# Token statistics two groups at a time, and an exchange of work between ScalarE and VectorE in a feed-forward block

## The chip, the cores and the metric

The kernel runs on one core of a Trainium2 chip as a single launch. The metric is device time in microseconds, the median of a few executions. A core has four compute engines with an instruction queue each, which works in order: TensorE (PE in the profile, its weight loads PEld), VectorE (DVE), ScalarE (ACT) and GpSimd (POOL). SyncE (SP) issues most DMAs. Engines wait for each other by semaphores alone.

## The reference

Two layers work on `x` of 64 images, 55 x 55 points, 96 channels.

```python
x = conv_out * x + bias + x                  # depthwise 25 x 25 taps, every third kept
t = x.reshape(64, 3025, 96)
t = t + attn(ln(t))                          # ln: mean and variance over the 96 channels
t = t + ffn(ln(t))
# attn: h = relu(bn1(t @ w1.T)); FFT over the 3025 tokens; an affine map and a relu on real and
#       imaginary part; inverse FFT; bn2(y @ w2.T)
# ffn:  h = relu(q16(q16(q8(t) @ q8(W1).T) + q8(b1))); q16(q16(q8(h) @ q8(W2).T) + q8(b2))
```

`q8` rounds to an 8-bit float with five exponent bits (fp8e5), `q16` to fp16. So in the feed-forward block (FFN) each matrix product is rounded to fp16, gets a bias, is rounded to fp16 again, and the hidden values are then rounded to fp8.

## The kernel before

The convolution comes first (to about 940 us): TensorE multiplies by Toeplitz matrices, VectorE and GpSimd finish the tiles, and the result goes to HBM. Then come 64 sequences, one per image. A sequence holds its 3025 tokens as 121 partitions x 25 groups x 96 channels in a tile `t`, laid out as two channel halves: `[121, 2, 25, 48]`.

Each sequence is a list of small tasks (`sequence`, from L334):

- load `t`; first layer norm: statistics of the 25 groups in five tasks (L350), then `layernorm_tasks` (L289); scale (L363, GpSimd), transpose (`pa`, L376), copy to SBUF (`tnt`, ACT), product with w1 (`ph`, L397) and relu (`h`, ACT), first DFT step (`pf`, L412), copy (`g`, ACT), a round trip through HBM (`gd` to `gt`)
- second DFT step (`px`, L478), three affine forms on ACT (L495), four comparisons on VectorE (L504) and two sums on GpSimd (L511), product with w2 (`pd`, L553, L563; copy `d` on ACT), inverse DFT (`pe`, L583; copy `e` on ACT; a round trip through HBM; `py`, L644), residual (L655, VectorE)
- second layer norm: statistics (L661), `layernorm_tasks` again, centre and quantise (`xc` L677, `xq` L686, GpSimd), transpose (`pq`, L695), copy (`tq`, ACT)
- FFN up, nine blocks of 128 hidden channels x 1008 tokens (1009 in the last third): product (`pu`, L718), cast to fp16 (`y16`, L727), bias and relu (`z16`, L730), quantise to fp8 (`hq`, L742)
- FFN down: product (`pw`, L762), cast (`o16`, ACT, L771), bias (L776, VectorE), residual (`ot`, L782, GpSimd), store.

The order of work is set by a planner, `ordered` (L134). Each task has an engine, a cost in us, tasks it follows, buffers that it makes and uses, and a place: its number in the list `PLACES` plus one per sequence. `ordered` plays the queues through with these costs and takes for each engine the ready task with the earliest place, within a margin; the tasks of all 64 sequences are then written out in the order of their planned starts. So a new cost or a new task list gives other orders on every engine. The SP queue takes its DMAs in the same order, and at the start of the sequences the last stores of the convolution are mixed in, one after every third task (L1097). `AHEAD` and `NAHEAD` (L52) say how many first tasks of the first two sequences are written out within the convolution: the load, the statistics and the layer norm.

Statistics: `bn_stats` sends 96 channels of one group through VectorE and writes six numbers: count, mean and sum of squared deviations of the even-numbered elements, and the same of the odd-numbered. GpSimd joins the two halves (`variance`, L295 to L306: five small instructions, and two more for the mean in the second layer norm). Then ScalarE takes the square root (L311) and variance plus epsilon (L312), VectorE inverts (L315), and GpSimd takes one Newton step in four instructions (L319 to L322).

Buffers that matter: `psw` gives two PSUM tiles for `px` and `pu`, `psn` four for all other products; `y16` and `z16` have two buffers each, `hq` one, `stc` one.

Of the kernel before, what the change touches and what calls it, by code (L numbers as in the profile page):

```python
# [14 lines left out]
AF = mybir.ActivationFunctionType  # L15
ALU = mybir.AluOpType
# [21 lines left out]
CHH = CH // 2  # L38
# [9 lines left out]
KH, KHP = 31, 32  # L48
KC = 8
UPT = 1008  # L50

AHEAD, NAHEAD = 2, 10  # L52
# [5 lines left out]
    -0.85, -0.814, -0.754, -0.694, -0.634, -0.574, -0.232, -0.28, -0.28, -0.28, -0.26146, -0.13246,  # L58
    -0.13246, 0, 0, 0.074, 0.05, 0.06623, 0.06623, 0.14023, 0.11623, 0.15385, -0.129, 0, 0, 0.13246,
    0.13246, 0.20646, 0.18246, 0.19869, 0.19869, 0.27269, 0.24869, 0.30769, 0.00346, 0.13246, 0.13246,  # L60
    0.26492, 0.26492, 0.33892, 0.31492, 0.33115, 0.33115, 0.40515, 0.38115, 0.46154, 0.13592, 0.26492,
    0.26492, 0.39738, 0.39738, 0.47138, 0.44738, 0.46361, 0.46361, 0.53761, 0.51362, 0.61538, 0.26838,
    0.39738, 0.39738, 0.52985, 0.52985, 0.60385, 0.57985, 0.59608, 0.59608, 0.67008, 0.64608, 0.76923,
    0.40085, 0.52985, 0.52985, 0.66231, 0.66231, 0.73631, 0.71231, 0.72854, 0.72854, 0.80254, 0.77854,
    0.92308, 0.53331, 0.66231, 0.66231, 0.79477, 0.79477, 0.86877, 0.84477, 1.07692, 0.72, 0.97, 1.22, 1.47,
    0.9, 0.9, 0.9, 0.9, 0.9, 0.9, 0.9, 0.9, 0.774, 0.774, 1.046, 1.046, 1.046, 1.046, 1.046, 1.046, 1.046,
    1.046, 0.92, 0.92, 1.192, 1.192, 1.192, 1.192, 1.192, 1.192, 1.192, 1.192, 1.066, 1.066, 1.514, 1.534,
    1.534, 1.584, 1.584, 1.584, 1.66, 1.68, 1.68, 1.73, 1.73, 1.73, 1.73333, 1.338, 1.338, 1.338, 1.338,
    1.338, 1.338, 1.338, 1.338, 1.212, 1.212, 1.484, 1.484, 1.484, 1.484, 1.484, 1.484, 1.484, 1.484, 1.358,
    1.358, 1.63, 1.63, 1.63, 1.63, 1.63, 1.63, 1.63, 1.63, 1.504, 1.504, 1.952, 1.972, 1.972, 2.022, 2.022,  # L70
    2.022, 2.098, 2.118, 2.118, 2.168, 2.168, 2.168, 2.23333, 2.477, 2.677, 2.677, 2.687, 2.743, 2.743,
    2.753, 2.809, 2.809, 2.819, 2.875, 2.875, 2.885, 2.941, 2.941, 2.951, 2.975, 2.927, 2.927, 2.927, 2.835,
    2.835, 3.235, 3.235, 2.856, 2.856, 3.256, 3.256, 2.877, 2.877, 3.277, 3.277, 2.898, 2.898, 3.298, 3.298,
    2.919, 2.919, 3.319, 3.319, 2.94, 2.94, 3.34, 3.34, 2.961, 2.961, 3.361, 3.361, 3.509, 3.54, 3.509,
    3.509, 3.59436, 3.62536, 3.59436, 3.59436, 3.67972, 3.71072, 3.67972, 3.67972, 3.78836, 3.81936,
    3.78836, 3.78836, 3.87372, 3.90472, 3.87372, 3.87372, 3.95908, 3.99008, 3.95908, 3.95908, 4.06772,
    4.09872, 4.06772, 4.06772, 4.15308, 4.18408, 4.15308, 4.15308, 4.23844, 4.26944, 4.23844, 4.23844,
    3.466, 3.466, 3.466, 3.266, 3.516, 3.74536, 3.74536, 3.74536, 3.54536, 3.79536, 3.83848, 3.83848,
    3.83848, 3.63848, 3.88848, 4.02472, 4.02472, 4.02472, 3.82472, 4.07472, 4.10232, 4.10232, 4.10232,
    3.90232, 4.15232,  # L80
# [4 lines left out]
def conv_attn_hybrid(ctx, tc, a, out, t1s, tb, gds, eds):  # L85
# [48 lines left out]
    def ordered(bufs):  # L134
# [93 lines left out]
        t=5, sta=2, stc=1, xa=2, tnt=2, h=3, g=3, gd=2, gt=4, m=2, ar=2, nc=2, d1=2, sm=3, sr=2, d=4, e=2, ed=2,  # L228
        e2=1, xc=2, xq=2, tq=1, hq=1, y16=2, z16=2, o16=2, ot=3, rstda=2, rstdc=2, mean=2, psn=4, psw=2,
# [59 lines left out]
    def layernorm_tasks(b, what, t, after, mean):  # L289
# [5 lines left out]
        def variance():  # L295
            st_ = live[st]
            d, v = box["d"], box["v"] = small("d", name), small("v", name)
            nc.gpsimd.tensor_tensor(d, st_[:, :, 1], st_[:, :, 4], ALU.subtract)
            nc.gpsimd.tensor_tensor(v, st_[:, :, 2], st_[:, :, 5], ALU.add)
            nc.gpsimd.tensor_tensor(d, d, d, ALU.mult)  # L300
            nc.gpsimd.tensor_scalar(d, d, CH / 4.0, None, ALU.mult)
            nc.gpsimd.tensor_tensor(v, d, v, ALU.add)
            if mean is not None:
                m = make(mean, "mean", [NJ, NR1])
                nc.gpsimd.tensor_tensor(m, st_[:, :, 1], st_[:, :, 4], ALU.add)
                nc.gpsimd.tensor_scalar(m, m, 0.5, None, ALU.mult)  # L306

        def root():
            v, s = box["v"], small("s", name)
            box["s"] = s  # L310
            nc.scalar.activation(s, v, AF.Sqrt, bias=eps, scale=1.0 / CH)  # L311
            nc.scalar.activation(v, v, AF.Identity, bias=eps, scale=1.0 / CH)  # L312
# [11 lines left out]
        new = [(mean, "mean")] if mean is not None else []  # L324
        k = task("POOL", 1.9 if new else 1.45, variance, after, new=new, use=[st])
        k = task("ACT", 0.57, root, [k])
# [3 lines left out]
    def sequence(b):  # L330
# [13 lines left out]
        for q in range(5):  # L344

            def stats(q=q):
                if q == 0:
                    make(sta, "sta", [NJ, NR1, 6])
                for g in range(5 * q, 5 * q + 5):
                    nc.vector.bn_stats(live[sta][:, g, :], live[t][:, :, g, :])  # L350

            after = [loaded] + ks[:1]
            new = [(sta, "sta")] if q == 0 else []
            ks.append(task("DVE", 0.8, stats, after, new=new, use=[t] if new else [t, sta]))
        rstd = layernorm_tasks(b, "a", t, ks, None)
# [284 lines left out]
        for q in range(5):  # L640
# [16 lines left out]
            def stats(q=q):  # L657
                if q == 0:
                    make(stc, "stc", [NJ, NR1, 6])
                for g in range(5 * q, 5 * q + 5):  # L660
                    nc.vector.bn_stats(live[stc][:, g, :], live[t][:, :, g, :])  # L661
# [5 lines left out]
            ks.append(task("DVE", 0.8, stats, [k] + ks[:1], new=new, use=[t] if new else [t, stc]))  # L667
        mean = ("mean", b)
        rstd = layernorm_tasks(b, "c", t, ks, mean)
        turned_ = []  # L670
        for i in range(7):
# [3 lines left out]
            def centre(xc=xc, g0=g0, ng=ng):  # L675
                x = make(xc, "xc", [NJ, 4, CH])
                nc.gpsimd.tensor_tensor(  # L677
                    halves(x[:, :ng]),
                    live[t][:, :, g0 : g0 + ng, :],
                    halves(spread(live[mean], g0, ng)),  # L680
                    ALU.subtract,
                )
# [21 lines left out]
            k = task("POOL", 0.9 if ng == 4 else 0.48, centre, [rstd], new=[(xc, "xc")], use=[t, mean])  # L704
# [4 lines left out]
        for s, k in np.ndindex(3, 3):  # L709
# [16 lines left out]
            def cast(pu=pu, y16=y16, n=n):  # L726
                nc.vector.tensor_copy(live[y16][:, :n], live[pu][:, :n])  # L727
# [11 lines left out]
            def quantised(s=s, k=k, n=n, n0=n0, z16=z16):  # L739
                if s == 0 and k == 0:  # L740
                    make(hq, "hq", None)
                nc.scalar.activation(  # L742
                    live[hq][:, k, n0 : n0 + n], live[z16][:, :n], AF.Copy, saturate=False
                )
# [3 lines left out]
            x = task("DVE", 1.14, cast, [x], use=[pu, y16])  # L748
# [478 lines left out]
```

## Time and profile before

| | |
|---|---|
| time, median of 3 runs | 4573.0 us (4572.97 to 4574.33) |
| the profiled execution | span 4570.5 us; the median stands 2.5 us over it |
| PE busy | 4227.5 us, 92% of the span |
| DVE, ACT, POOL busy | 3311.5, 2953.9, 3071.1 us (72, 65, 67%) |
| y16 cast, L727, DVE | 576 instructions, 1201 ns each |
| z16 bias, L730, DVE | 576, 731 ns |
| hq quantise, L742, ACT | 576, 1049 ns |
| statistics, L350 and L661, DVE | 3200, 242 to 243 ns |
| mean granted TensorE clock | 0.974 of full speed |

Busy time is the union of an engine's instructions. Consecutive instructions of an engine overlap a little in the records, so the distance from start to start is what one costs its queue. "Idle before" is the time an engine stood still ahead of an instruction, with what released it; "issue" is idle time in which it waited for nothing that the profile shows. The chain of waits goes back from the last instruction, at each step to what released it.

### The profile page before, as it was taken

Reading aid. Unit: us, or ns where it says so; the run is one execution under the profiler, and the core shown is the slowest. Engines: PE = TensorE matmul, PEld = TensorE weight load, DVE = VectorE, ACT = ScalarE, POOL = GpSimd, SP = SyncE. Lnnn points to the kernel's source line nnn. Section 1 sums busy time; section 2 is a strip of 40 time slices with the busy share of each in tenths; the row PEclk is TensorE's granted clock in tenths of the full one; section 3 lists DMA queues with packets and bytes.
Section 4 is the critical chain, followed back from the end, with each engine's and each line's share of the span. In section 5 each row is a group of like instructions: output and inputs, shape, how many; then the busy total and the mean of one; then the engine's idle time right before and its main releaser. Section 6 shows DMA issues by size and latency. Waiting matters only on the chain.

```text
span 4570.5 us, 194901 instructions
## 1 busy us (share of the span) xinstructions
PE 4227.5 (92%) x83314; PEld 3487.6 (76%) x83314; DVE 3311.5 (72%) x7344; ACT 2953.9 (65%) x5947; POOL 3071.1 (67%) x4196
## 2 busy tenths in 40 slices
PE   8999898949999999999999999999999999999996
PEld 8989898937777777777777777777777777777774
DVE  5444344424788888888788788888888888888877
ACT  2000000017788888888888888888888888888875
POOL 2667676725666777777677676677777777667765
PEclk9999999969999999999999999999999999999996
DMA  4788888876666666766666666666666666667662
GB/s 178 180 206 207 247 197 196 198 171 168 167 176 177 177 180 179 186 179 178 178 181 182 177 175 179 177 180 179 177 182 181 184 182 177 179 175 181 178 173 79
DMA packets 572901, 823.11 MB, mean 180 GB/s; under 512 B 61641, under 2 KB 470924, under 8 KB 570754
## 3 DMA queue, kind: packets, MB, share of 16 engines
q1 hardware_dynamic: 449094, 741.40, 60.0%
q10 hardware_dynamic: 107996, 60.19, 7.0%
q0 software_dynamic: 14944, 9.06, 1.1%
q8 instruction: 655, 10.73, 1.0%
q14 instruction: 212, 1.74, 0.1%
HBM read 419.45 MB, written 390.64 MB: 177 GB/s over the span
## 4 chain that ended last, share of the span: by engine, by line
PE 62%; DVE 9%; DMA 9%; ACT 8%; issue 6%; POOL 4%; SPq 2%; ACTq 1%; POOLq 0%; DVEq 0%
PE pl L1000 13%; PE pf L412 9%; PE ph L397 8%; PE px L478 6%; PE pd L553 6%; PE py L644 4%; PE pu L718 3%; PE pd L563 3%; PE pe L583 3%; PE pa L376 2%; DMA x<-in_xc_dram 2%; PE pw L762 2%; DVE y L727 2%; POOL xq L686 1%; ACT m L495 1%
## 5 line engine op out<-in xcount | busy, mean ns | idle before, releaser
L1000 PE MATMUL pl<-x,toep 128*64 128x96 f32 (+1 forms) x18432 | 793.3, 250 | 75.4 <-DVE buf L1008 30.9
L1000 PEld LDWEIGHTS pl<-x,toep 128*64 128x64 f32 (+1 forms) x18432 | 785.8, 137 | 82.7 <-DVE buf L1008 32.0
L727 DVE CAST y<-pu 128x1008 f16<-128x1008 f32 (+1 forms) x576 | 688.6, 1201 | 197.7 <-PE pu L718 195.3
L397 PEld LDWEIGHTS ph<-w1e,tnt 97*121 97x121 f32 x3200 | 546.1, 185 | 247.5 <-issue 65.5
L397 PE MATMUL ph<-w1e,tnt 97*121 97x192 f32 x3200 | 670.1, 332 | 44.1 <-ACT g L416 26.4
L742 ACT ACTIVATE hq<-z 128x1008 fp8e5<-128x1008 f16 (+1 forms) x576 | 600.6, 1049 | 163.5 <-DVE z L730 162.9
L412 PE MATMUL pf<-h,f 121*128 121x384 f32 (+1 forms) x1664 | 667.9, 486 | 22.6 <-ACT h L406 16.0
L504 DVE SCALAR_TENSOR_TENSOR m<-px,par,m 128x400 f32<-128x400 f32 x768 | 480.7, 626 | 261.6 <-ACT ar L495 183.7
L311 ACT ACTIVATE sm_s_a<-sm_v_a,eps 121x25 f32<-121x25 f32 x64 | 20.4, 318 | 898.3 <-DMA t<-buf 876.3
L363 POOL TENSOR_TENSOR xa<-shared,rstda 121x384 f32<-121x384 f32 (+1 forms) x364 | 283.2, 781 | 366.7 <-PE pa L376 360.8
L478 PE MATMUL px<-m,gt 50*64 50x50 f32 x24576 | 453.0, 220 | 48.8 <-issue 42.9
L511 POOL TENSOR_TENSOR sm<-ar,m 128x400 f32<-128x400 f32 x256 | 269.9, 1054 | 339.0 <-DVE m L504 294.6
L478 PEld LDWEIGHTS px<-m,gt 50*64 50x64 f32 x24576 | 413.7, 135 | 107.7 <-issue 90.1
L1008 DVE SCALAR_TENSOR_TENSOR buf<-pl,x 121x384 f32<-121x384 f32 (+1 forms) x336 | 270.9, 842 | 291.8 <-PE pl L1000 176.9
L416 ACT COPY g<-pf 128x384 f32<-128x384 f32 (+1 forms) x832 | 385.8, 468 | 127.1 <-PE pf L412 62.7
L1018 POOL TENSOR_TENSOR buf<-buf,cbias 121x768 f32<-121x768 f32 (+1 forms) x168 | 303.4, 1819 | 237.2 <-DVE buf L1008 184.9
L553 PE MATMUL pd<-w2e,sm 128*64 128x96 f32 x8192 | 412.7, 252 | 33.3 <-ACT g L416 19.4
L406 ACT ACTIVATE h<-ph 121x384 f32<-121x384 f32 (+1 forms) x832 | 389.5, 488 | 66.5 <-PE ph L397 59.5
L730 DVE TENSOR_SCALAR z<-y,b1q 128x1008 f16<-128x1008 f16 (+1 forms) x576 | 418.2, 731 | 11.3
L553 PEld LDWEIGHTS pd<-w2e,sm 128*64 128x64 f32 x8192 | 354.5, 138 | 79.6 <-ACT g L416 23.9
L412 PEld LDWEIGHTS pf<-h,f 121*128 121x128 f32 x1664 | 293.3, 192 | 93.0 <-ACT h L406 24.0
L782 POOL TENSOR_TENSOR ot<-shared,o 121x480 f32<-121x480 f32 x260 | 304.3, 1178 | 81.2 <-DVE o L776 81.2
(129 smaller groups left out, 8639.3 us busy)
## 6 DMA issues: line engine op xcount, KB each, us to landing
gd<-g SPq DMA_DIRECT2D x768, 192.0 KB
gt<-gd SPq DMA_DIRECT2D x512, 288.0 KB
x<-in_xc_dram SPq DMA_DIRECT2D x240, 384.0 KB
out_dram<-ot SPq DMA_DIRECT2D x320, 210.0 KB
ed<-e SPq DMA_DIRECT2D x384, 150.0 KB
shared<-t SPq DMA_DIRECT2D x52, 1050.0 KB
t<-buf ACTq DMA_DIRECT2D x137, 288.0 KB
t<-shared ACTq DMA_DIRECT2D x65, 288.0 KB
```

The source lines that it names most:

```text
L397: nc.tensor.matmul(x[:NJ, q * H : (q + 1) * H], live[tnt][:, g * NJ : (g + 1) * NJ], w1e, start=True, stop=True,)
L406: nc.scalar.activation(live[h][:, : nq * H], live[ph][:NJ, : nq * H], AF.Relu)
L412: nc.tensor.matmul(x[:, : nq * H], f1, live[h][:, : nq * H], start=True, stop=True)
L416: nc.scalar.copy(live[g][:, q0 : q0 + nq].rearrange("p q c -> p (q c)"), live[pf][:, : nq * H])
L478: nc.tensor.matmul(x[to : to + 64].rearrange("p (q r n) -> p q r n", q=2, r=2)[:, k2p, :, o : o + NR1], y[rows, k % KC, c0 : c0 + 64], m1[ ...
L504: nc.vector.scalar_tensor_tensor(live[out_], view(px)[:, :, 256 : 256 + KC * NR1], scale, live[than], ALU.mult, ALU.max)
L553: nc.tensor.matmul(y[k % 2][64 * k2p : 64 * k2p + 64, k // 2 * CH : (k // 2 + 1) * CH], full[:, k, 64 * k2p : 64 * k2p + 64], w2e[:, 0, :] ...
L727: nc.vector.tensor_copy(live[y16][:, :n], live[pu][:, :n])
L730: nc.vector.tensor_scalar(make(z16, "z16", [128, 1024], F16)[:, :n], live[y16][:, :n], b1q[:, k : k + 1], 0.0, ALU.add, ALU.max,)
L742: nc.scalar.activation(live[hq][:, k, n0 : n0 + n], live[z16][:, :n], AF.Copy, saturate=False)
L782: nc.gpsimd.tensor_tensor(halves(y), live[t][:, :, 5 * q : 5 * q + 5], halves(live[o16]), ALU.add)
L1000: nc.tensor.matmul(pl[p : p + width, cc * NBS : (cc + 1) * NBS], toep[:, c0 + g + cc, o : o + width], xts[n, c0, m + d][:, g + cc, :], sta ...
```

## The change

1. Statistics take two groups per instruction. The access pattern runs over channels and, innermost, over the two groups, so that even elements belong to one group and odd ones to the other: 13 instructions of 192 elements in place of 25 of 96. The 25th group is paired with itself. Mean and sum of squares then come out per group, and the tile is `[121, 26, 3]`.
2. `variance` goes from both layer norms. ScalarE's `root` reads the sums straight from the statistics tile, and `centre` on GpSimd reads the mean there. `stc` gets a second buffer, `mean` goes, `PLACES` loses the two entries of `variance`, and `NAHEAD` is 9 for 10.
3. FFN up: ScalarE casts `pu` from PSUM to fp16, and VectorE quantises `z16` to fp8. The bias between them stays on VectorE.
4. The planner's costs follow: the five statistics tasks 0.56 or 0.84 us for 0.8, `root` 0.45 for 0.57, the cast 0.95 (ACT) for 1.14 (DVE), the quantise 0.62 (DVE) for 0.95 (ACT).

```diff
-AHEAD, NAHEAD = 2, 10
+PAIRS = ((0, 2), (2, 5), (5, 7), (7, 10), (10, 13))
+AHEAD, NAHEAD = 2, 9
...
+    def pair_stats(st, t, i):
+        g0, ng = 2 * i, min(2, NR1 - 2 * i)
+        x = t[:, :, g0 : g0 + ng, :].rearrange("p h g c -> p h c g")
+        if ng == 1:
+            x = x.to_broadcast([NJ, 2, CHH, 2])
+        nc.vector.bn_stats(st[:, g0 : g0 + 2, :].rearrange("p g n -> p (g n)"), x)
...
-        def variance():
...
         def root():
-            v, s = box["v"], small("s", name)
-            box["s"] = s
-            nc.scalar.activation(s, v, AF.Sqrt, bias=eps, scale=1.0 / CH)
-            nc.scalar.activation(v, v, AF.Identity, bias=eps, scale=1.0 / CH)
+            m2 = live[st][:, :NR1, 2]
+            v, s = box["v"], box["s"] = small("v", name), small("s", name)
+            nc.scalar.activation(s, m2, AF.Sqrt, bias=eps, scale=1.0 / CH)
+            nc.scalar.activation(v, m2, AF.Identity, bias=eps, scale=1.0 / CH)
...
-        k = task("POOL", 1.9 if new else 1.45, variance, after, new=new, use=[st])
-        k = task("ACT", 0.57, root, [k])
+        k = task("ACT", 0.45, root, after, use=[st])
...
-                for g in range(5 * q, 5 * q + 5):
-                    nc.vector.bn_stats(live[stc][:, g, :], live[t][:, :, g, :])
+                for i in range(*PAIRS[q]):
+                    pair_stats(live[stc], live[t], i)
...
-                    halves(spread(live[mean], g0, ng)),
+                    halves(spread(live[stc][:, :, 1], g0, ng)),
...
-                nc.vector.tensor_copy(live[y16][:, :n], live[pu][:, :n])
+                nc.scalar.copy(live[y16][:, :n], live[pu][:, :n])
...
-                nc.scalar.activation(
-                    live[hq][:, k, n0 : n0 + n], live[z16][:, :n], AF.Copy, saturate=False
-                )
+                nc.vector.tensor_copy(live[hq][:, k, n0 : n0 + n], live[z16][:, :n], saturate=False)
...
-            x = task("DVE", 1.14, cast, [x], use=[pu, y16])
+            x = task("ACT", 0.95, cast, [x], use=[pu, y16])
...
-            hq_done[s, k] = task("ACT", 0.95, quantised, after, new=[(hq, "hq")] if first else [], use=[z16] if first else [z16, hq])
+            hq_done[s, k] = task("DVE", 0.62, quantised, after, new=[(hq, "hq")] if first else [], use=[z16] if first else [z16, hq])
```

## The prediction

> **What bounds the kernel now.** First the page, for how much of the span each engine works and what the chain that ended last is made of:
>
> ```profile
> PE 4227.5 (92%) x83314; PEld 3487.6 (76%) x83314; DVE 3311.5 (72%) x7344; ACT 2953.9 (65%) x5947; POOL 3071.1 (67%) x4196
> ...
> PE 62%; DVE 9%; DMA 9%; ACT 8%; issue 6%; POOL 4%; SPq 2%; ACTq 1%; POOLq 0%; DVEq 0%
> ```
>
> The change touches only the 64 sequences, so the stage is looked at alone. The table of windows (length, then busy time of PE, PEld, DVE, ACT, POOL, granted clock, DMA share, GB/s):
>
> ```profile
> 940.00:1000.00 60.00, 24.60 (x89) 18.62 (x89) 15.20 (x93) 12.97 (x32) 14.06 (x39) 0.66 0.76 167
> ...
> 2000.00:2500.00 500.00, 476.75 (x9069) 374.95 (x9068) 409.27 (x940) 417.18 (x841) 355.37 (x530) 1.00 0.69 179
> 2500.00:3000.00 500.00, 475.96 (x9160) 375.08 (x9160) 413.38 (x958) 417.48 (x842) 355.28 (x530) 0.99 0.68 179
> ...
> 4500.00:4570.50 70.50, 43.32 (x354) 26.78 (x346) 49.12 (x85) 36.21 (x56) 39.34 (x52) 0.65 0.24 73
> ```
>
> In the steady part TensorE is busy 95% of the time, ACT and DVE 83%, POOL 71%. From 1000 to 4500 us there are 556 casts L727, nine to a sequence: 61.8 sequences, 56.6 us each. The change takes no work from TensorE, so only its idle time can be won. Who ended that, by the waits from 1000 to 4500 us (total us, times, longest), and the longest waits of the other engines there:
>
> ```profile
> PE px L478 <- issue: 42.9, 52, 2.4
> PE pd L553 <- ACT g L416: 19.4, 30, 0.8
> ...
> PE ph L397 <- ACT e L592: 11.4, 29, 0.4
> PE pa L376 <- ACT g L416: 10.0, 1, 10.0
> ...
> ACT hq L742 <- DVE z L730: 146.5, 179, 4.1
> ...
> POOL sm_d_c L298 <- DVE stc L661: 74.3, 61, 8.6
> ```
>
> PE's waits that name "issue" come to 87 us (px 42.9, pd 15.4 and 11.8, pe 8.1, pw 5.3, pq 3.0); they often fall in the middle of a run of matmuls and no part of the change touches them. Waits for ACT come to 60 us (g 19.4 and 3.3, e 11.4, o 7.8 and 3.1, h 6.2, hq 3.4, d 3.3, tq 1.7, without the single 10.0), for POOL 7, for DVE some 9. Why ACT is late, a stretch of the chain of waits shows (start, us, what):
>
> ```profile
> 2033.37 0.97 DVE o L776
> 2034.35 1.12 DVE y L727
> 2035.47 0.56 DVE shared L655
> 2036.03 0.62 DVE z L730
> 2036.65 0.02 issue
> 2036.68 1.05 ACT hq L742
> ...
> 2039.33 0.49 ACT e L592
> 2039.82 0.04 issue
> 2039.87 0.91 PE ph L397 x4
> ```
>
> VectorE is late with the bias, ACT stands in `hq` for it, and the PSUM copies queued behind `hq` reach TensorE late. And the bias is late because of GpSimd, by the timeline:
>
> ```profile
> 2023.13 0.83 POOL L363 TENSOR_TENSOR xa<-shared,rstda 121x384 f32<-121x384 f32 x1
> 2023.17 1.06 DVE L730 TENSOR_SCALAR z<-y,b1q 128x1008 f16<-128x1008 f16 x1
> ```
>
> `z` starts 0.04 us after `xa` and ends 0.27 us after it, though its shortest record is 374 ns. Over the steady part `z` takes 0.48 us on average when it starts with POOL idle, 0.83 when POOL is at work (worked out from the timeline): it waits for the running GpSimd instruction.
>
> **The change, part by part**, per sequence of 56.6 us.
>
> *Statistics.* Ten `bn_stats` of a run take 1.69 us in the timeline and five 0.89: 0.16 us from start to start for 96 elements. DVE's rows of 400 and 1008 elements step by 0.54 and 1.12 us, 0.95 ns an element, so a pair of 192 takes 0.16 + 96 x 0.95 = 0.25 us. 50 x 0.16 = 8.0 us become 26 x 0.25 = 6.5: DVE -1.5. No row shows the pattern that jumps between two groups; should it run at half rate, a pair takes 0.43 us and the term is +3.2. I take full rate, since `residual` and `centre` already read split patterns at ordinary rates.
>
> *Variance and mean.* The ten rows L298 to L306 of the two norms come to 88.4 + 115.9 = 204 us: POOL -3.2 us. The path from the last statistics to the root loses 1.6 us. POOL's wait for `stc` (74.3 us, 1.2 a sequence) goes over to ACT, where `root` now waits for VectorE directly; before, the root started 2.3 us after the statistics. Behind it on ACT stand `h`, `g`, `d` and `o`, for which PE waits. Price 0 to 1.2 us of ACT; I take 0, as the planner moves `root` with its inputs, and keep 1.2 for the range.
>
> *Cast on ACT.* ACT's PSUM rows: `o` 564 ns for 480 elements; slopes 0.78 (tnt, 484 against 121) to 0.91 ns (h, 384 against 192). So 0.98 to 1.04 us for 1008, against 1.05 for `hq`: ACT -0.6 to 0. ACT no longer waits for `z` (146.5 us, 2.4 a sequence); it waits for `pu`, and through the two `y16` buffers for the `z` two blocks earlier.
>
> *Quantise on DVE.* The nearest rows are two fp8 casts from SBUF in the preparation, 384 elements 342 ns and 288 elements 291 ns: 0.53 ns an element and 138 fixed, 0.67 us for 1008, 0.59 from start to start. That it moves two elements per cycle suggests that it shuts GpSimd out, and is shut out, as `z` is. Bounds of its wait: 0 (POOL idle) and 1.05 us (a whole POOL row such as L511). `z` waits 0.36 (731 less 374); but the changed order puts `hq` directly behind its `z` in 352 of 576 cases, where POOL, held up by `z`, gets in between. The nearest row for that is `z` directly behind a bias L776: 0.87 us, a wait of 0.50. I take 0.5 to 0.6. Nine times: cast -9 x 1.12 = -10.1, quantise +9 x (0.59 + 0.55) = +10.3. DVE +0.2, from -4.8 to +4.7.
>
> *Sums.* DVE -1.3, ACT -0.3, POOL -3.2 plus what `hq` makes it stand (0 to 9 x 0.59 x 0.71 = 3.8; half of it, 1.9) = -1.3. No engine becomes the bound. The gain is in who waits for whom: ACT, which feeds TensorE, is cut loose from the VectorE to GpSimd contention, and `hq` on VectorE is needed only by `pw`, which waited 3.4 us in all. I take half of the 60 us that PE waits for ACT, since one of ACT's four large waits goes and the chain passes through it: -30 us. All of it, with POOL's 7, would be -67; nothing, 0.
>
> *A rule of the Trainium skill against this.* The row first: `z` above ends with the POOL instruction, 374 ns at best and 1326 at worst. "SBUF — State Buffer", section "Who interferes with whom", says the same as a rule: VectorE's two-port instructions and GpSimd hold a port pair exclusively for a whole instruction, and ScalarE never waits for anyone; so the move takes work from the engine that can't be blocked to one that can. By the rule's half of a POOL instruction the nine quantises would cost VectorE 9 x (0.59 + 0.5 x 0.71 x 1.0) = 8.5 us, by the row behind L776 10.3.
>
> *Ends.* From 940 to 1025 us the chain stands in SP's DMA queue (L1100) and PE does nothing; the same stores precede the first complete set of `gd` puts, with two of them later in between: 0, plus or minus 3. In the last 70 us the root comes 1.6 us earlier, and the last six FFN blocks, which step by 1.12 + 0.39 us on DVE, step by 0.39 + 0.59 there and 0.9 on ACT: 6 x 0.5 = 3.2. Some of it is lost to POOL: -4 (0 to -8).
>
> 4570.5 - 30 - 4 = 4536.5; with the 2.5 us by which the median stands over the span, **4539 us**, 0.7% faster.
>
> **The rivals.**
>
> - *Hidden anyway.* PE's idle time hardly moves, since what ended last was a tie of several late engines; the tail alone remains: 4573 - 5 = 4568. For it: TensorE is at 95%, and half of its idle time is "issue". Against: the chain through `hq` above.
> - *The contention decides: slower.* Place: the pairs `z`, `hq` on VectorE. VectorE's time stands even at a wait of (10.1 + 1.5) / 9 - 0.59 = 0.70 us per `hq`. At a whole POOL row, 1.05, it has 9 x 0.35 = 3.2 us more; `z` falls behind, `y16` is not free, ACT stands in the cast and PE behind ACT. One POOL row of 0.83 us (L363) on PE per sequence is 62 x 0.83 = +51: 4624. For it: after the change VectorE has 23 instructions a sequence that contend, for 14. Against: POOL has 3.2 us less to do.
> - *Another order, by chance worse.* All queues are planned anew with the old places. If PE's 1.2 us of waits on engines per sequence double, 76 us: 4649. Nothing in the profile speaks for a sign.
> - *The fp8 copy runs at one element per cycle.* Then 9 x 0.5 = 4.5 us more on DVE, as in the second rival; the two preparation rows speak against it.
>
> **How the numbers follow.** The forecast 0.52, hidden anyway 0.16, contention 0.22 (the slow copy in it), a worse order 0.10. About 0.2%, 9 us, is what a measurement tells from no change. Faster: 0.52 and a quarter of the hidden case, 0.56; within it: the rest of that, 0.12; slower: 0.32. The likeliest case alone runs from 4573 - 75 = 4498 (all 67 and 8 of the tail) to 4564. The range goes below it by a little, for waits that the view counts under other names, to 4492, and up to 4624, the price of contention, leaving the worse orders out: 0.05 below and 0.13 above.
>
> **What would show it.** `bn_stats` x1664 near 335 ns a record; `hq` on DVE 0.67 us at its shortest and 1.1 to 1.3 on average; the cast on ACT near 1.0; no wait ACT hq for DVE z; PE above 96% in the steady windows, and its waits for ACT near 30 us. It is wrong if ACT's cast waits for VectorE, if `root` waits for `stc` by more than 50 us in all, if `hq` averages over 1.45 us, or if PE's waits on DVE, 9 us now, grow past 40.

## The result: 5.6% slower, and the profile after

The changed kernel takes 4833.6 us (median; 4828.1 to 4835.3) against 4573.7 us beside it: a ratio of 1.056, 95% interval 1.0528 to 1.0592. The forecast was 4539 us, its range ended at 4624. Sign and range were both wrong. The profiled execution has a span of 4833.5 us, 263 us more than before.

The page of the changed kernel: the span, the busy times, and what the chain that ended last is made of.

```profile
span 4833.5 us, 192945 instructions
...
PE 4315.1 (89%) x83314; PEld 3562.8 (74%) x83314; DVE 3006.5 (62%) x5808; ACT 2933.5 (61%) x5947; POOL 2994.2 (62%) x3428
...
PE 61%; issue 9%; POOL 8%; DMA 8%; ACT 6%; DVE 5%; SPq 2%; ACTq 1%; POOLq 0%; DVEq 0%
```

DVE, ACT and POOL all have less to do than before (3311.5, 2953.9, 3071.1 us), and yet the whole takes longer. In the chain, POOL has doubled (4 to 8%), "issue" went from 6 to 9%. TensorE has the same 83314 matmuls and is busy 88 us more. The table of windows of the changed kernel (length, busy time of PE, PEld, DVE, ACT, POOL, granted clock, DMA share, GB/s) shows that it is the steady part that lost:

```profile
940.00:1000.00 60.00, 26.78 (x87) 19.44 (x86) 10.83 (x40) 12.95 (x32) 5.41 (x10) 0.66 0.78 150
2000.00:2500.00 500.00, 449.15 (x8373) 354.58 (x8371) 341.71 (x679) 381.72 (x774) 317.27 (x388) 0.96 0.63 163
2500.00:3000.00 500.00, 450.95 (x8175) 355.72 (x8172) 338.81 (x672) 376.10 (x765) 313.04 (x384) 0.95 0.64 164
```

TensorE's busy share fell from 95 to 90%, and its granted clock from 0.99 or 1.00 to 0.95 or 0.96. At the start of the sequences (940 to 1000 us) TensorE is about as busy as it was (26.78 us, 24.60 before). From 1100 to 4400 us a sequence (nine `z` records) takes 59.64 us, before 55.10. Of these 4.54 us, 3.02 are idle time of TensorE (5.61 for 2.59) and 1.52 are busy time (54.03 for 52.51); sixty times 4.54 us, 272 us, covers the whole loss. (The prediction's 56.6 us a sequence was an average that took in the slow start; it scaled only small terms.)

Who ended TensorE's idle time in the changed kernel, from 1050 to 4750 us (total us, times, longest):

```profile
PE px L472 <- issue: 101.9, 65, 4.7
PE pq L689 <- POOL xq L680: 42.0, 66, 1.5
PE pe L577 <- issue: 32.3, 21, 4.7
PE pw L754 <- DVE hq L736: 31.6, 32, 3.9
...
PE pd L547 <- ACT g L410: 8.0, 11, 1.2
```

Summed by releaser, and set against the kernel before from 1050 to 4500 us: "issue" 182 us (before 87), GpSimd 51 (7), VectorE 51 (11), ScalarE 51 (55). So three kinds of wait grew, and the waits for ScalarE, of which half should have gone, hardly moved.

The durations of the changed instructions, in contrast, came out close to what was foreseen or below it. Groups of VectorE in the changed kernel (busy us, mean ns of one, then the idle time ahead of them with its releasers):

```profile
L736 DVE CAST hq<-z 128x1008 fp8e5<-128x1008 f16 (+1 forms) x576 | 508.4, 886 | 12.5
...
L724 DVE TENSOR_SCALAR z<-y,b1q 128x1008 f16<-128x1008 f16 (+1 forms) x576 | 379.0, 661 | 348.6 <-ACT y L721 348.2
...
L295 DVE BATCH_NORM_STATS2 stc<-shared 121x6 f32<-121x192 f32 x676 | 197.9, 350 | 0.8
```

From the list of ScalarE's waits there, its `y16` cast (`y`), a copy (`tnt`) and the root of the second layer norm (`sm_s_c`):

```profile
ACT y L721 <- PE pu L712: 21.8, 28, 3.0
ACT tnt L375 <- PE pa L370: 15.6, 22, 1.6
ACT sm_s_c L306 <- DVE stc L295: 7.5, 10, 1.1
```

The cast is not held by VectorE, and that root waits 7.5 us for `stc` in all. The local steps of the change did what was expected of them; the whole did not.

### The profile page after: what moved, and what is told of

The parts are those of the page before. It is cut to its first block, busy times and chain, and to the rows that moved or that the text cites. A ratio compares the mean times of both kernels' runs of the same rounds, so it can differ in the third digit from the quotient of the medians.

```text
span 4833.5 us, 192945 instructions
## 1 busy us (share of the span) xinstructions
PE 4315.1 (89%) x83314; PEld 3562.8 (74%) x83314; DVE 3006.5 (62%) x5808; ACT 2933.5 (61%) x5947; POOL 2994.2 (62%) x3428
## 4 chain that ended last, share of the span: by engine, by line
PE 61%; issue 9%; POOL 8%; DMA 8%; ACT 6%; DVE 5%; SPq 2%; ACTq 1%; POOLq 0%; DVEq 0%
PE pl L992 12%; PE pf L406 8%; PE ph L391 7%; PE pd L547 7%; PE px L472 6%; PE py L638 4%; PE pd L557 4%; PE pu L712 3%; PE pe L577 3%; PE pw L754 3%; PE pa L370 3%; DMA x<-in_xc_dram 2%; DMA gt<-gd 2%; POOL xq L680 2%; POOL ot L774 2%
## 5 line engine op out<-in xcount | busy, mean ns | idle before, releaser
L992 PE MATMUL pl<-x,toep 128*57 128x96 f32 (+1 forms) x18432 | 790.3, 249 | 73.0 <-DVE buf L1000 32.4
L992 PEld LDWEIGHTS pl<-x,toep 128*57 128x57 f32 (+1 forms) x18432 | 781.6, 136 | 81.5 <-DVE buf L1000 33.5
L721 ACT CAST y<-pu 128x1008 f16<-128x1008 f32 (+1 forms) x576 | 581.5, 1013 | 29.5 <-PE pu L712 26.6
L724 DVE TENSOR_SCALAR z<-y,b1q 128x1008 f16<-128x1008 f16 (+1 forms) x576 | 379.0, 661 | 348.6 <-ACT y L721 348.2
L306 ACT ACTIVATE sm_s_a<-sta,eps 121x25 f32<-121x25 f32 x64 | 22.2, 347 | 880.2 <-DMA t<-buf 871.0
L736 DVE CAST hq<-z 128x1008 fp8e5<-128x1008 f16 (+1 forms) x576 | 508.4, 886 | 12.5
L410 ACT COPY g<-pf 128x384 f32<-128x384 f32 (+1 forms) x832 | 399.1, 481 | 136.5 <-PE pf L406 79.5
L547 PE MATMUL pd<-w2e,sm 128*64 128x96 f32 x8192 | 435.4, 261 | 42.2 <-issue 13.8
L547 PEld LDWEIGHTS pd<-w2e,sm 128*64 128x64 f32 x8192 | 377.1, 145 | 100.0 <-issue 37.0
L566 ACT COPY d<-pd 128x384 f32<-128x384 f32 x512 | 220.6, 483 | 316.0 <-PE pd L557 315.3
L680 POOL TENSOR_TENSOR xq<-xc,rstdc 121x384 fp8e5<-121x384 f32 (+1 forms) x448 | 367.9, 832 | 51.3 <-PE pq L689 50.0
```

The lines of the kernel that those rows point to most:

```text
L410: nc.scalar.copy(live[g][:, q0 : q0 + nq].rearrange("p q c -> p (q c)"), live[pf][:, : nq * H])
L547: nc.tensor.matmul(y[k % 2][64 * k2p : 64 * k2p + 64, k // 2 * CH : (k // 2 + 1) * CH], full[:, k, 64 * k2p : 64 * k2p + 64], w2e[:, 0, :] ...
L680: nc.gpsimd.tensor_tensor(x[:, :ng], live[xc][:, :ng], spread(live["rstdc", b], g0, ng), ALU.mult, saturate=False)
L721: nc.scalar.copy(live[y16][:, :n], live[pu][:, :n])
L724: nc.vector.tensor_scalar(make(z16, "z16", [128, 1024], F16)[:, :n], live[y16][:, :n], b1q[:, k : k + 1], 0.0, ALU.add, ALU.max,)
L736: nc.vector.tensor_copy(live[hq][:, k, n0 : n0 + n], live[z16][:, :n], saturate=False)
```

## The experiments

Two theories stood first. One: the changed operations cost the time (the contention rival of the prediction, by whatever path). Two: the order costs it, because every queue was planned anew from places that had been set for the old costs and tasks. An order and the operations in it can be taken apart here: if the planner is given the old costs and task list, the old order is written out, and the task bodies may still issue the new instructions on the new engines.

### All of the new operations in the old order

```diff
 # costs, task list, PLACES, buffer counts as the planner sees them: those of the kernel before
+        def variance():
+            pass
-        k = task("ACT", 0.45, root, after, use=[st])
+        k = task("POOL", 1.9 if new else 1.45, variance, after, new=new, use=[st])
+        k = task("ACT", 0.57, root, [k])
```

> All operations of the changed kernel, written out in the order that the planner made for the kernel before (it plans with the old task list, engines and costs; the two variance tasks stand in the plan and issue nothing). Order theory (the queues planned anew cost the time, the operations do not): 4540 to 4600 us. Contention theory (the fp8 quantise on VectorE and GpSimd hold each other up, so the operations cost the time): 4780 to 4850 us, as the changed kernel. TensorE's waits in the middle of a run of matmuls under issue: order theory about 80 us, as before; contention theory no statement.

Measured: 4689 us, ratio 1.0246 (1.021 to 1.0282). So 2.5% belongs to the operations even in the order that suited the kernel before, and the new order adds 1.056 / 1.0246 = 1.031, another 3.1%. The time lies between the two windows that were expected, and both theories hold a part. In this run TensorE waited 79.5 us for `xq` on GpSimd (6.9 before).

### The old operations in the new order

```diff
 # costs, task list and PLACES: those of the changed kernel
-                nc.scalar.copy(live[y16][:, :n], live[pu][:, :n])
+                nc.vector.tensor_copy(live[y16][:, :n], live[pu][:, :n])
-                nc.vector.tensor_copy(live[hq][:, k, n0 : n0 + n], live[z16][:, :n], saturate=False)
+                nc.scalar.activation(live[hq][:, k, n0 : n0 + n], live[z16][:, :n], AF.Copy, saturate=False)
 # root issues the five or seven GpSimd instructions of variance as before; bn_stats one group at a time
```

> The operations of the kernel before, written out in the order that the planner made for the changed kernel (variance stands directly ahead of the root). Order theory: 4780 to 4900 us, about as slow as the changed kernel or slower, as the casts are on an engine the plan did not mean. Contention theory: 4560 to 4640 us.

Measured: 5221 us, ratio 1.1408 (1.1345 to 1.1471), with a granted clock of 0.932. That is above both windows. The order made for the exchange is much worse for the old operations than for the new ones. The shares of order and operations therefore do not simply add: an order is good or bad for one assignment of work.

### The changed kernel with another margin of the planner

```diff
-    FULL, SWITCH, NEAR, RING = "128x128", 0.09, 0.359, 8
+    FULL, SWITCH, NEAR, RING = "128x128", 0.09, 0.2, 8
```

> The changed kernel with one number of the planner changed: the margin by which a ready task may run ahead of one with an earlier place, 0.2 for 0.359. All operations and costs stay; only the order differs. Order theory: the time moves by more than 40 us either way from 4834, and TensorE's idle time in the steady part moves with it. Contention theory: 4800 to 4870 us, since the same operations meet each other as often.

Measured: 4681 us (the median of 4654, 4681 and 4685; a fourth execution of 18392 us stands apart and is not in the ratio), ratio 1.0198 (1.0135 to 1.0261). One constant of the planner, with no instruction changed, wins 150 us back. So an order alone can carry some 3.5% (1.056 / 1.0198 = 1.035), no less than the step from the old order to the new one; the changed operations then take about what they take in the old order (1.0246).

### The kernel before with its margin moved

```diff
-    FULL, SWITCH, NEAR, RING = "128x128", 0.09, 0.359, 8
+    FULL, SWITCH, NEAR, RING = "128x128", 0.09, 0.37, 8
```

> The kernel before with the planner's margin 0.37 for 0.359; all operations and costs stay, only the order differs. If the order before was a fortunate one that any new planning loses: 4650 to 4850 us. If the order matters little: 4560 to 4610 us.

Measured: 4798 us, ratio 1.046 (1.0417 to 1.0504). Moving the margin by 0.011 costs the unchanged operations 4.6%. So the order of the kernel before is a fortunate one for its places: a small step of the margin leaves it. Only this one step was tried.

### The FFN exchange alone, in the old order

```diff
-                nc.vector.tensor_copy(live[y16][:, :n], live[pu][:, :n])
+                nc.scalar.copy(live[y16][:, :n], live[pu][:, :n])
-                nc.scalar.activation(
-                    live[hq][:, k, n0 : n0 + n], live[z16][:, :n], AF.Copy, saturate=False
-                )
+                nc.vector.tensor_copy(live[hq][:, k, n0 : n0 + n], live[z16][:, :n], saturate=False)
```

> The kernel before with the exchange in the feed-forward block alone (cast on ScalarE, quantise on VectorE) and with the order and statistics of before. Order theory: 4540 to 4610 us. Contention theory: 4750 us or more, as nothing of GpSimd's work has gone.

Measured: 4683 us, ratio 1.0232 (1.0196 to 1.0269): nearly all of the 2.5% is the exchange. The time lies between the windows of the two theories. TensorE's longest waits in this run, 1050 to 4500 us:

```profile
PE pq L695 <- POOL xq L686: 76.3, 108, 2.0
PE px L478 <- issue: 37.6, 44, 2.2
```

Before, the first of these was 6.9 us. Its cause stands in GpSimd's groups, same operations and same order, first in this run and then in the kernel before (1100 to 4400 us; the number after the busy time is the mean ns of one):

```profile
L686 POOL TENSOR_TENSOR xq<-xc,rstdc 121x384 fp8e5<-121x384 f32 x354 | 312.7, 890 | 1.4 <-PE pq L695 0.8 <-DMA gt<-gd 0.6
...
L511 POOL TENSOR_TENSOR sm<-d,nc 128x400 f32<-128x400 f32 x234 | 266.8, 1140 | 0.0
L363 POOL TENSOR_TENSOR xa<-shared,rstda 121x384 f32<-121x384 f32 x276 | 258.5, 939 | 239.8 <-PE pa L376 237.8 <-DMA gd<-g 0.2
```

```profile
L686 POOL TENSOR_TENSOR xq<-xc,rstdc 121x384 fp8e5<-121x384 f32 x362 | 305.9, 851 | 7.8 <-PE pq L695 7.6
...
L511 POOL TENSOR_TENSOR sm<-d,nc 128x400 f32<-128x400 f32 x240 | 248.5, 1035 | 0.0
L363 POOL TENSOR_TENSOR xa<-shared,rstda 121x384 f32<-121x384 f32 x291 | 247.9, 852 | 299.5 <-PE pa L376 293.8 <-PE pu L718 2.9
```

These three rows are 39 to 105 ns longer. Within this one trace the longer records are those that meet an `hq` in time: `sm` takes 1038 ns on average beside neither `hq` nor `z`, 1030 ns beside a `z` alone and 1480 ns beside an `hq` alone (137, 42 and 55 records, by the times of start and end). Per sequence the durations of GpSimd's records add up to 43.3 us for 40.4, +2.9. It works through `xc` and `xq` in one stretch, in which it hardly waits (1.4 us ahead of `xq` in all), and the transposes `pq` follow right behind it: there 1.2 of the 2.9 us a sequence turn into TensorE's wait. TensorE's idle time is 3.70 us a sequence for 2.59, and a sequence takes 56.79 us for 55.10. The exchange did also what it was forecast to do: TensorE's waits for ScalarE fell, from 54.5 to 30.7 us. But its waits for GpSimd rose from 6.9 to 76.3.

### The exchange with a quantise of 16 columns

```diff
-                nc.vector.tensor_copy(live[hq][:, k, n0 : n0 + n], live[z16][:, :n], saturate=False)
+                nc.vector.tensor_copy(live[hq][:, k, n0 : n0 + 16], live[z16][:, :16], saturate=False)
```

This kernel is the one above, but quantises 16 of the 1008 columns of each block; the rest of `hq` is zero.

> As the run with the exchange alone in the old order (4683 us), but the quantise on VectorE handles 16 of the 1008 columns of each block; the rest of hq stays zero, so most of the quantise is left out. Every task, wait and place in the queues stays. Contention theory (hq keeps GpSimd off SBUF for 0.6 us, GpSimd's xq comes late and TensorE waits for it in the transpose): 4540 to 4600 us, TensorE's wait of pq for xq back from 76 us to under 25. Misplaced-cast theory (ScalarE's queue suffers since the cast stands where the plan had VectorE's): 4650 to 4700 us, the wait stays above 50.

Measured: 4634 us, ratio 1.0103 (1.006 to 1.0147), above the 4540 to 4600 of the contention theory. GpSimd's records are back at 40.45 us a sequence, and the wait is nearly gone, as that theory expected:

```profile
PE px L478 <- issue: 53.8, 53, 2.9
...
PE pq L695 <- POOL xq L686: 13.4, 25, 1.2
```

So the full-width quantise costs 1.3 of the exchange's 2.3%, and it does so by making GpSimd stand, or by the time it takes of VectorE. The next run is meant to tell these apart.

### The same with VectorE kept busy otherwise

```diff
+                nc.vector.tensor_reduce(
+                    live[z16][:, :320], live[z16][:, :320].unsqueeze(2), axis=AX.X, op=ALU.max
+                )
                 nc.vector.tensor_copy(live[hq][:, k, n0 : n0 + 16], live[z16][:, :16], saturate=False)
```

> As the run before, with an extra VectorE instruction on 320 columns of z16 (a maximum over one element, which changes nothing and moves one element per cycle) ahead of the 16 columns: VectorE spends about as long on a block as with the whole quantise, but holds nothing that GpSimd needs for longer. The quantise is left out but for 16 columns. Contention theory: within 25 us of the run with 16 columns alone, xq's wait still under 35 us. VectorE-time theory (it is the longer VectorE time, not GpSimd being held): 4650 to 4700 us.

Measured: 4654 us, ratio 1.0148 (1.0109 to 1.0188); the wait of `pq` for `xq` is 12.6 us from 1050 to 4500 us, as without the extra work. The time alone decides nothing, as it lies in the windows of both theories (within 25 us of the run before, and 4650 to 4700); the wait speaks for the contention theory. The intervals of this run and the one before it overlap, so VectorE's time is worth some 0.4%, if anything, and makes no wait for `xq`; from here to the whole quantise it is 1.0232 / 1.0148, 0.8%. The comparison is not exact: VectorE is busy 41.0 us a sequence here, 38.4 with 16 columns alone and 42.6 with the whole quantise. The wait for `xq` comes with the quantise that holds GpSimd up.

About 1% of the exchange is left when the quantise is small, and its cause stays open. In the run with 16 columns alone `z` waits 512 us for the cast, which now stands in ScalarE's queue at a place meant for VectorE; that this wait is the 1% was not tried. TensorE's waits for "issue" are also longer there, 113 us for 87.

### The statistics alone, in the old order

```diff
-                for g in range(5 * q, 5 * q + 5):
-                    nc.vector.bn_stats(live[stc][:, g, :], live[t][:, :, g, :])
+                for i in range(*PAIRS[q]):
+                    pair_stats(live[stc], live[t], i)
 # variance issues nothing; root and centre read the statistics tile; planned as before
```

> The kernel before with the new statistics alone (pairs, no variance or mean on GpSimd), written out in the old order; the feed-forward block is untouched. Order theory: 4550 to 4580 us, the same or a little faster, since GpSimd loses 3.2 us and VectorE 1.3 us of work per sequence and neither is the bound. If the strided pairs or the direct wait of the root for VectorE cost anything, 4590 or more.

Measured: 4601 us, ratio 1.0034 (1.0018 to 1.0049). GpSimd's records lose 3.0 us a sequence (40.4 to 37.4), and the time does not fall, though 4550 to 4580 us were expected. In the old order this time of GpSimd is off the path. TensorE's idle time is 3.03 us a sequence for 2.59; that is "issue" (121 us for 87 from 1050 to 4500 us), while its waits for the other engines fell from 72 to 62 us.

### Each part alone, planned anew

```diff
 # statistics alone: the changed kernel with cast on VectorE, quantise on ScalarE, and their old costs
-            x = task("ACT", 0.95, cast, [x], use=[pu, y16])
+            x = task("DVE", 1.14, cast, [x], use=[pu, y16])
 # exchange alone: the kernel before with
-            x = task("DVE", 1.14, cast, [x], use=[pu, y16])
+            x = task("ACT", 0.95, cast, [x], use=[pu, y16])
```

> The change's statistics alone (pairs, no variance on GpSimd), FFN as before, planned anew with the changed kernel's list of places. Theory A (the new order carries about 3% of the loss, whichever operations stand in it): the same operations in the old order took 4601 us, ratio 1.003; planned anew they land far above it, 4700 to 4850 us, ratio 1.03 to 1.06, with TensorE's waits spread over several inputs. Theory B (the loss is the FFN exchange's own, and its order only carries it): within 0.7% of the old order, 4590 to 4630 us.

> The FFN exchange alone, statistics as before, planned anew with the old list of places. In the old order these operations took 4683 us, ratio 1.023. Theory A (any new order under the old places is worse by some 3%): 4720 to 4850 us. Theory B (the planner knows the exchanged costs, so a plan made for them should win back what the old order loses): at or under 4683 us, pq's wait for GpSimd xq under 40 us (75.8 in the old order).

Measured: 4765 us, ratio 1.0387 (1.0344 to 1.043), for the statistics; 4826 us, ratio 1.0519 (1.0464 to 1.0575), for the exchange. Both lie in the windows of the theory that a new order costs time. Planning anew under the old places costs the statistics 1.0387 / 1.0034 = 3.5%, the exchange 2.8%, both together 3.1%. The exchange's wait for `xq` did fall to 30.2 us, as its rival expected, and other waits took its place (`px` for issue 81.5, `pw` for `hq` 44.6), so the time rose. With the statistics, which have no exchange in them, the waits are others again:

```profile
PE pd L547 <- ACT g L410: 89.2, 68, 2.8
PE px L472 <- issue: 28.2, 29, 2.8
PE pa L370 <- POOL xa L357: 25.5, 19, 1.4
```

### All three assignments with an order fitted to them

The comparison so far favours the kernel before, which alone has an order made for it. So the places and the margin were fitted to each assignment: places were shifted at random in groups, and a shift was kept if the planner's own play-through ended earlier; its costs of `z`, of the output bias and of `hq` were set near what they take.

```diff
 PLACES = (
-    ...
+    ...
 )
-    FULL, SWITCH, NEAR, RING = "128x128", 0.09, 0.359, 8
+    FULL, SWITCH, NEAR, RING = "128x128", 0.09, 0.5, 8     # statistics; 0.18 all; 0.395 before
-            x = task("DVE", 0.4, bias, [x], new=[(z16, "z16")], use=[y16])
+            x = task("DVE", 0.6, bias, [x], new=[(z16, "z16")], use=[y16])
```

> All of the changed kernel's operations, with the list of places and the planner's margin fitted anew to them (and the planner's costs of z, of the output bias and of hq set to what they took: 0.6, 0.66 and 0.85). Theory A (order is 3.1 of the 5.6%, the operations' own price 2.5%): a fitted order wins back the order's part and a little of the price, 4600 to 4690 us, so still above the kernel before. Rival (the operations are worth having, and only the order hid it): under 4565 us.

> The statistics of the change alone, FFN as before, places and margin fitted anew in the same way. GpSimd and VectorE have 3 and 1.5 us a sequence less to do than in the kernel before, and the exchange is absent. Theory A (order decides): 4480 to 4620 us; at its good end it beats both kernels. Rival (TensorE bounds at 95% and the old order is already as good as these operations allow): 4570 to 4600 us, as in the old order. If it lands above 4650 us, the planner's model is no guide to the order, and that is the finding.

> The kernel before, with nothing of the change, places and margin fitted anew in the same way as for the statistics alone (4523 us, ratio 0.986). Theory A (GpSimd and VectorE relieved by the statistics leave room that a fitted order turns into time): within 0.5% of the kernel before, 4560 to 4610 us. Rival (the fit alone did it, the statistics are worth nothing): 4500 to 4545 us.

| assignment, with an order fitted to it | us | ratio to the kernel before |
|---|---|---|
| the kernel before | 4578 | 0.9966 (0.9944 to 0.9988) |
| the statistics alone | 4523 | 0.9862 (0.9831 to 0.9893) |
| all of the change | 4705 | 1.0251 (1.0203 to 1.0298) |

The statistics with their own order beat both kernels, by 1.4% and 6.6%. Fitting alone is worth 0.3%, so 0.9862 / 0.9966, some 1.0%, lies between the statistics and the kernel before, each with one order fitted to it. That the relief of GpSimd and VectorE is what wins this 1.0% is not shown: from 1100 to 4400 us TensorE waits for other engines and DMAs 29 us in the one and 17 us in the other, and for "issue" 95 and 157 us. A sequence takes 54.10 us for 55.51, and "issue" makes 1.1 of these 1.4 us. So a luckier order of the same matmuls may be a good part of it. All of the change lands a little above the window that was expected of it (4600 to 4690); with the one order that was fitted to it the exchange is not worth having. The page of the statistics with fitted places:

```profile
PE 4202.9 (93%) x83314; PEld 3491.2 (77%) x83314; DVE 3227.9 (72%) x5808; ACT 2945.4 (65%) x5947; POOL 2887.5 (64%) x3428
...
PE 74%; DMA 10%; ACT 7%; issue 4%; SPq 2%; POOL 1%; ACTq 1%; DVE 1%; POOLq 0%; DVEq 0%
```

Three quarters of the chain is TensorE's own work (62% in the kernel before), GpSimd and VectorE have nearly left it. The waits for ScalarE that the exchange was to remove come to 14 us here from 1100 to 4400 us, for 51 in the kernel before, without an exchange. In the kernel before with fitted places they come to 12 us, so an order can remove them without any part of the change.

### The exchange in the fitted order of the statistics

```diff
 # planned and written out as the statistics with fitted places
-                nc.vector.tensor_copy(live[y16][:, :n], live[pu][:, :n])
+                nc.scalar.copy(live[y16][:, :n], live[pu][:, :n])
-                nc.scalar.activation(
-                    live[hq][:, k, n0 : n0 + n], live[z16][:, :n], AF.Copy, saturate=False
-                )
+                nc.vector.tensor_copy(live[hq][:, k, n0 : n0 + n], live[z16][:, :n], saturate=False)
```

> The statistics with fitted places, planned and written out exactly as in the run of 4523 us; then the cast stands on ScalarE and the quantise on VectorE, in that same order. Theory A (the exchange costs what its instructions do: GpSimd held up, VectorE loaded, the cast late; 2.3% in the old order): 4600 to 4650 us, ratio to the kernel before 1.004 to 1.016, pq's wait for GpSimd xq at 20 to 70 us (3.3 without the exchange) and GpSimd's own xc and xq again 4% longer. Rival (2.3% was the ill fit of the old order to the exchange): 4510 to 4560 us.

Measured: 4704 us, ratio 1.024 (1.0212 to 1.0267), so 1.024 / 0.9862 = 3.8% for the exchange, more than expected. The page's chain, and below it TensorE's first waits from 1050 to 4500 us:

```profile
PE 51%; POOL 18%; DMA 11%; issue 10%; ACT 5%; SPq 2%; DVE 2%; ACTq 1%; POOLq 0%; DVEq 0%
```

```profile
PE pq L694 <- POOL xq L685: 136.1, 209, 1.3
PE px L477 <- issue: 47.5, 45, 2.7
```

GpSimd's records add up to 39.99 us a sequence for 37.02, again +3.0, and its share of the chain goes from 1 to 18%. The wait for `xq`, 3.3 us without the exchange, is 136. TensorE's idle time is 4.53 us a sequence for 2.25, and this wait is as large as the whole difference. The rest of the 3.46 us that a sequence is longer stands in TensorE's busy time (53.03 for 51.85), 0.74 of it in the records of `pq` itself. The same mechanism stands in both orders, in one of which GpSimd had been relieved. With an order fitted to it the exchange costs about as much (1.0251 / 0.9862 = 3.9%), then in other waits: `pa` for `xa` 25.5 us, `pq` for `xq` 16.8, and `px` for its `gt` loads 49.0.

## Why the prediction was wrong, point by point

- **The durations were near, and were not what failed.** The pair of `bn_stats` takes 350 ns (335 forecast), the cast on ScalarE 1013 (980 to 1040), `hq` 610 at its shortest (670). `hq` averages 0.89 us, less than the 1.1 to 1.3 foreseen. The sum of GpSimd's records fell by 1.4 us a sequence (39.0 for 40.4; 1.3 forecast) and ScalarE's by 0.3 (20.4 us over 64; 0.3 forecast). VectorE's busy time fell by more than the 1.3 forecast: 305 us over 64, 4.8. Of the difference 2.4 us are `hq`, which takes 7.9 us a sequence for 10.3 foreseen.
- **"I take half of the 60 us that PE waits for ACT: -30 us"** is the term of the sum that failed as a whole. In the changed kernel these waits are 51 us for 55. The mechanism exists: in the old order the exchange took those waits from 54.5 to 30.7 us. But it was made the balance of the exchange, when a second row belonged on the same line: in that run TensorE's waits for GpSimd went from 6.9 to 76.3.
- **GpSimd's loss was sized, and then not followed.** The estimate was 1.9 us a sequence with a bound of 3.8; it is 2.9 and 3.0 in the two runs that take the exchange alone in an unchanged order. The step that failed is what came next: "-1.3", so "no engine becomes the bound". GpSimd's gain (the variance) and its loss (the quantise) were added, as if they were the same time. They lie in different places: the variance in a place off the path (relieving GpSimd by 3.0 us won nothing in the old order), the loss in the stretch `xc`, `xq`, ahead of `pq`, where GpSimd works without a pause and TensorE follows close. "For POOL 7" in the waits before was read as slack of little interest. A wait of 20 short pieces, 0.8 us at most, whose releaser works without a pause in that stretch, meant that GpSimd was just in time.
- **"The contention decides: slower" had the right engine pair and the wrong path.** It let VectorE fall behind and pass the delay on through `y16` and ScalarE. In fact `hq` cost VectorE less than foreseen (0.89 us on average, 0.61 at its shortest: a wait of some 0.28), ScalarE's cast never waited for VectorE, and the delay went through GpSimd. So its condition (a wait of over 0.70 us per `hq`) was not met, and its price, +51, was low: the exchange alone costs 2.3% in the old order, 106 us.
- **"Another order, by chance worse: nothing in the profile speaks for a sign"** is the second step that failed, in chance (0.10) and size (+76). The new order costs 3.1%, some 140 us, and the price left out "issue", of which TensorE's waits doubled (87 to 182 us), and the clock. Set against the same operations in the old order, a sequence takes 59.64 us for 56.90; of these 2.74 us, 1.25 are "issue" and 1.08 TensorE's busy time, at a granted clock of 0.962 for 0.987. There was a reason for a sign: an order is fitted to one assignment, and five new orders under old or moved places (both parts, each part, the margin at 0.37, and the old operations in the new order) were worse by 2.8 to 14%. The one that was better, the margin at 0.2, only won back what the new order had lost.
- **"No part of the change touches" the waits for issue:** wrong as well. The order does; see below.
- **"`hq` on VectorE is needed only by `pw`, which waited 3.4 us in all"** held in orders that had not been planned for the exchange (no such wait in the first of the two runs, 0.3 us in the second). In the changed kernel `pw` waits 31.6 us for `hq`, and 44.6 us with the exchange alone planned anew. With it the prediction's own sign of being wrong came: TensorE's waits for VectorE went from 11 to 51 us, past 40.
- The skill's rule that was weighed ("SBUF — State Buffer", "Who interferes with whom") spoke against the change and was right in direction. The prediction used it for what VectorE loses. It speaks of an exclusive lock, which works both ways, and the runs show the price that TensorE paid on the other side: GpSimd's 2.9 us a sequence. VectorE's own wait, nine times 0.28 us, is an estimate of 2.5 us, and in the old order TensorE's waits for VectorE stayed at 11 us.
- *Hidden anyway* and the slow fp8 copy did not happen; the start at 940 us did not move, as forecast.

## What to carry to other kernels

When work moves to an engine that shares a resource, follow the delay of its neighbour too, to the first consumer that has no slack: a wait that is short, frequent, and released by an engine that works without a pause in the stretch ahead of it marks such a place. Gains and losses of an engine are not one sum unless they lie in the same stretch of its queue. Where an order of work has been fitted to the operations, judge a change of operations in the old order and again with an order fitted to it: here the statistics looked 0.3% slower in the old order and were 1.0% faster with fitted orders on both sides, while the exchange cost 2.3% in the old order and 3.9% with a fitted one. One fitted order for each is a small sample: an order is worth some per cent by itself, and part of such a difference can be its luck.

## What the hardware showed that was not expected

**Instruction loads stop TensorE.** Its queue of instruction loads on the page of the changed kernel:

```profile
q8 instruction: 655, 10.73, 0.9%
```

That is 655 packets of 16384 bytes for 166628 matmuls and weight loads, one packet for about 256 of them. Every stall over 0.25 us inside a run of equal matmuls that the trace puts down to "issue" (91 in the kernel before from 1100 to 4480 us, 103 in the changed one) lies a multiple of 256 instructions after the last, give or take two, and one such packet lands 1.2 to 1.7 us before TensorE goes on. The same spacing of 256 stands in the traces of all the experiments, where these stalls make 86% or more of TensorE's waits for "issue" from 1100 to 4400 us. One of them in the timeline of the changed kernel (start, us, what, idle before):

```profile
3485.09 1.90 PE L472 MATMUL px<-m,gt 50*64 50x50 f32 x115
3491.69 0.57 PE L472 MATMUL px<-m,gt 50*64 50x50 f32 x11 [4.71 <-issue]
```

No wait for an input ended there: it stopped after 115 of 126 `px` and went on 1.5 us after its packet of instructions (3489.17 to 3490.23). Such stalls come only where the last 256 instructions took under 7.7 us, half of them under 4.1: runs of small `px`, `pd`, `pe` matmuls that stand close together. Most such stretches pass without a stall. Per stall the mean is 0.9 us before and 1.6 in the changed kernel (82 and 163 us in all), so the order decides how dear they are. Why the loads come later in the one than in the other is open.

**After a pause of TensorE the clock often stands at a half, even after one of 2 us.** The windows around that stall of 4.7 us, changed kernel (granted clock third from the end):

```profile
3484.00:3488.00 4.00, 2.99 (x159) 2.74 (x155) 1.76 (x2) 2.54 (x5) 4.00 (x6) 1.00 0.94 264
3488.00:3492.00 4.00, 0.31 (x12) 0.31 (x16) 3.51 (x9) 0.15 (x1) 0.86 (x2) 0.73 0.59 173
3492.00:3496.00 4.00, 4.00 (x59) 3.65 (x51) 0.69 (x3) 2.41 (x6) 1.61 (x3) 0.50 0.19 49
3496.00:3500.00 4.00, 4.00 (x16) 2.40 (x16) 3.28 (x9) 3.36 (x8) 2.13 (x3) 0.50 0.27 99
3500.00:3504.00 4.00, 4.00 (x73) 3.34 (x72) 1.64 (x5) 2.03 (x5) 0.61 (x1) 0.99 0.96 255
```

After it the clock is 0.50 for some 10 us. From 1100 to 4400 us the clock stood at a half for 253 us in 47 spells of 3.4 to 10.2 us, before for 38 us in 10. Half of the difference, 108 us, is what it can cost, and TensorE's 1.52 us more a sequence (55 of them: 84 us) fit under that; so idle time of TensorE can have been paid for again as slow work. That all 84 us are the clock's is not shown, since busy time also grew in a run whose clock did not change (53.03 us for 51.85, above). The Trainium skill has a rule for the clock ("TensorE: Matmul & The Clock Gate", section "What's actually happening"): an idle window of about 3.4 us drops the clock to a half. All 11 idle gaps of 3 us and more in the changed kernel (3.07 to 4.71) were followed by such a spell, in agreement with it. But so were 19 of 27 gaps of 2 to 3 us, 11 of 27 of 1.5 to 2 us, and 8 of 50 of 1 to 1.5 us: here idle gaps shorter than the rule's window were enough in many cases. The kernel before had 9 gaps of 2 us or more (20 us in all), the changed one 38 (109 us).
